# Inverse square roots by power on GpSimd, adjacency scaled once per graph, and the norms' last instruction on ScalarE

## The chip, the cores and the metric

The kernel runs on one core of one Trainium2 chip. The core has five engines that work at once, each through its own instructions in their order: TensorE (PE in the profile, its weight loads PEld), VectorE (DVE), ScalarE (ACT), GpSimd (POOL) and SyncE (SP), which here issues every DMA. What is measured is the device time of one launch in microseconds (us); less is better.

## The reference

64 graphs of N = 256 nodes with D = 128 features and a symmetric 0/1 adjacency with ones on its diagonal go through four layers. Every layer is followed by a residual and a layer norm without gain.

```
norm(v)  = (v - mean(v)) / sqrt(var(v) + 1e-5)            # over the 128 features
x1 = norm(x  + max_j adj[i,j] * relu(x_i (W1-W2) + x_j W2 + b))
x2 = norm(x1 + tanh([adj @ elu(x1 Win), elu(x1 Wnode), adj^T @ elu(x1 Wout)] @ Wupd + b))
A  = dinv_i * (adj + I) * dinv_j,   deg_i = sum_j adj[i,j] + 1,   dinv = deg^-1/2 where deg > 0, else 0
x3 = norm(x2 + A @ (elu(A @ (elu(elu(x2 W0 + b0)) W1) + b1) W2) + b2)
msg[i,j] = gelu(norm(x3_j Wa + x3_i Wb + b) * g1 + be1);  agg_i = sum_j adj[i,j] * msg[i,j]
z  = norm([x3, agg] @ W2 + b2) * g2 + be2
out = norm(x3 + z)
```

So there are five norms per graph: those that give x1, x2, x3 and out have no gain, the one that gives z has gain and offset. Layer 4 has in addition one inverse root for each message, a pair (i, j) of neighbours.

## The kernel before

Features or nodes lie on the 128 partitions; H = 2 halves of 128 nodes make a graph. The function `sparse` does the work; `general` is a second path that is entered only when a graph does not fit `sparse`'s tables, and in the measured runs it is not entered. A function such as `layernorm` is a Python generator: at each `yield` another may go on.

**Stages.** Four stages work on four successive graphs at once: `first` (layer 1), `second` (layer 2), `third` (layer 3, and the first four message tiles of layer 4) and `last` (the rest of layer 4 and the output). `together` takes steps of the four in turn, weighted by their number of steps: `STAGES = [(last, 34), (third, 34), (second, 14), (first, 44)]`. In the order in which the steps are taken, the instructions go into the engines' queues. All 64 graphs are unrolled.

**Layer 4.** Neighbours are packed into columns: WIDTH = 4800 columns for each half, cut into tiles of 1024, the last of 704, so that a graph has ten tiles (`TODO`). `sums_of` makes a tile: PE multiplies into `bigp` (L728), DVE adds `dT` into `pre` (L732), ACT squares (L736), PE sums over the features (L743), ACT writes the variances as `row` (L745), and SP sends `row` to a `line` in DRAM (L750). Each second tile (`GROUP = 2`) the group's variances come back spread over the partitions, as `vr` with 16 numbers on each of 128 (or 108) partitions (L762), and a mask `fu` (L764). `inverse_root` takes the square root on ACT and the reciprocal on DVE (L74, L75); L769 multiplies by the mask; L771 sends `vr` to `scale_line`. `last` fetches that, spread over all partitions, as `rs_s` (L828), two tiles ahead; DVE multiplies `pre` by it (L839), ACT takes the Gelu (L841), and DVE's `fold` adds it up (L492). There are 320 groups: five for each graph.

**Norms.** `layernorm` takes statistics on DVE (L171, L172), adds 1e-5 on DVE (L174), takes the root on ACT and the reciprocal on DVE (L74, L75) and then writes each half with one DVE instruction, subtract and multiply (L180), or two with a gain (L184, L185).

**Layer 3.** `layer_2` makes `deg` and `dinv` (root on ACT, reciprocal on DVE), adds the unit matrix to `aT` (L277), and in each of its two steps scales both halves of `hs` by `dinv` on DVE (L293) just ahead of the matrix products with `aT` (L296). The result is scaled by `dinv` of the other side in L308. `deg` comes from `dg`, a tile that `first` has left in `state`.

**ACT's tables.** ACT holds one set of functions at a time. Where the next activation needs another, an instruction ACT_TABLE_LOAD stands ahead of it, and the trace gives it the line of that activation: L74 (square root), L841 (Gelu), L194 and L198 (Exp of `elu`), L254 (Tanh).

Of the kernel before, what the change touches and what calls it, by code (L numbers as in the profile page):

```python
# [9 lines left out]
F32 = mybir.dt.float32  # L10
BF16 = mybir.dt.bfloat16
AF = mybir.ActivationFunctionType
# [31 lines left out]
def kernel(  # L44
# [26 lines left out]

    def inverse_root(t):

        nc.scalar.activation(t, t, AF.Sqrt)  # L74
        nc.vector.reciprocal(t, t)  # L75
# [81 lines left out]
    class Shared:  # L157
# [8 lines left out]
        def layernorm(self, dst, src, g=None, be=None):  # L166

            st = self.work.tile([P, H, 6], F32, name="st", bufs=4)
            mv = self.work.tile([P, H, 2], F32, name="mv", bufs=4)
            for h in range(H):  # L170
                nc.vector.bn_stats(st[:, h], src[:, h])  # L171
                nc.vector.bn_aggr(mv[:, h], st[:, h])  # L172
            rs = self.work.tile([P, H], F32, name="rs", bufs=4)
            nc.vector.tensor_scalar(rs, mv[:, :, 1], EPS, None, ALU.add)  # L174
            yield
            inverse_root(rs)
            yield
            for h in range(H):
                if g is None:
                    nc.vector.tensor_scalar(  # L180
                        dst[:, h], src[:, h], mv[:, h, 0:1], rs[:, h:h + 1], ALU.subtract, ALU.mult
                    )
                else:
                    nc.vector.scalar_tensor_tensor(dst[:, h], src[:, h], mv[:, h, 0:1], g, ALU.subtract, ALU.mult)  # L184
                    nc.vector.scalar_tensor_tensor(dst[:, h], dst[:, h], rs[:, h:h + 1], be, ALU.mult, ALU.add)  # L185
# [17 lines left out]
        def to_features(self, xn, name, bufs=None):  # L203

            pt = self.psum()
            for h in range(H):
                nc.tensor.transpose(pt[:, h * P:(h + 1) * P], xn[:, h], ident)
            t = self.state.tile([P, N], F32, name=name, **({"bufs": bufs} if bufs else {}))
            nc.scalar.copy(t, pt[:, :N])
            return t  # L210

# [49 lines left out]
        def layer_2(self, s, aT, deg_of):  # L261
# [3 lines left out]
            deg = work.tile([P, H], F32, name="deg")  # L265
            deg_of(deg)
            nc.vector.tensor_scalar(deg, deg, 1.0, None, ALU.add)
            pos = work.tile([P, H], F32, name="pos")
            nc.vector.tensor_scalar(pos, deg, 0.0, None, ALU.is_gt)
            dinv = work.tile([P, H], F32, name="dinv")  # L270
            nc.vector.tensor_scalar(dinv, deg, 1e-30, None, ALU.max)
            inverse_root(dinv)
            yield
            nc.vector.tensor_mul(dinv, dinv, pos)
            for h in range(H):
                blk = aT[:, h, h * P:(h + 1) * P]
                nc.vector.tensor_add(blk, blk, ident)  # L277
            yield
# [12 lines left out]
            for step in (1, 2):  # L291
                for h in range(H):
                    nc.vector.tensor_scalar(hs[:, h], hs[:, h], dinv[:, h:h + 1], None, ALU.mult)  # L293
# [60 lines left out]
    def sparse(ctx):  # L354
# [147 lines left out]
        def first(g, s):  # L502
# [40 lines left out]
            dg = state.tile([P, H], F32, name="dg", bufs=3)  # L543
            nc.vector.tensor_reduce(dg, pc, AX.X, ALU.add)
            s["dg"] = dg
# [172 lines left out]
        def sums_of(s, i):  # L718
# [50 lines left out]
            nc.vector.tensor_mul(vr[:rows], vr[:rows], fu[:rows])  # L769
# [12 lines left out]
        def third(g, s):  # L782

            dg = s["dg"]

            def deg_of(deg):
                nc.vector.tensor_scalar(deg, dg, 1.0 / N, None, ALU.mult)

            yield from sh.layer_2(s, s["aT"], deg_of)
# [105 lines left out]
    def general(ctx):  # L895
# [82 lines left out]
        def middle(g, s):  # L978
# [10 lines left out]
            def deg_of(deg):  # L989
                nc.vector.tensor_reduce(deg, an, AX.X, ALU.add)  # L990

            yield from sh.layer_1(s, an, aT, s["x1"])
            yield
            yield from sh.layer_2(s, aT, deg_of)
# [148 lines left out]
```

## Time and profile before

| | |
|---|---|
| median of 3 runs | 5732.73 us (5721.88 to 5733.99) |
| the profiled execution, its own time | 5731.62 us |
| its span, first to last instruction | 5729.7 us |
| mean granted TensorE clock | 0.862 |
| busy: PE, DVE, ACT | 4529.9, 4834.4, 4275.2 us |
| busy: POOL | 1.9 us, 10 instructions |

The page gives, for each engine, its busy time and share of the span; then the span in slices; the DMA queues; the chain of work that ended last, which is followed back from the last instruction; and the costliest groups of instructions. A group's line reads: line, engine, operation, output<-input, the shape, xcount, then busy us and mean ns of one, then the idle time of the engine just ahead of it, with what ended that. Busy shares are averages over stretches with different limits. So the table of stretches (the windows view), which gives each engine's busy time in any stretch of the span, is used as well, with the timeline and the list of waits (who waited for whom, us in total, times, longest).

### The profile page before, as it was taken

The numbers are of one execution on the slowest core, as the hardware profiler recorded it, in microseconds if no ns is written. First come the engines' busy times: TensorE is split into PE (matmuls) and PEld (weight loads), VectorE is DVE, ScalarE is ACT, GpSimd is POOL, SyncE is SP. The second block draws the span as 40 slices with busy tenths as digits, with TensorE's granted clock in tenths as the row PEclk, the third lists the DMA queues.
The fourth block names the chain that finished last, engine by engine and source line by source line (L and its number), as shares of the span: only waits on it lengthen the run. The fifth ranks groups of instructions, "written<-read, shape, count | busy, mean of one in ns | idle before, by whom it ended". The sixth has DMA issues, their size and how long they took to land.

```text
span 5729.7 us, 83531 instructions
## 1 busy us (share of the span) xinstructions
PE 4529.9 (79%) x27408; PEld 2508.7 (44%) x27408; DVE 4834.4 (84%) x14654; ACT 4275.2 (75%) x6485; POOL 1.9 (0%) x10
## 2 busy tenths in 40 slices
PE   5878878878778778788788788787887887877875
PEld 2444444444444444444444444444444444444443
DVE  6788888888888888888888888888888888888876
ACT  2577777777777777777777777777777777777785
POOL 0000000000000000000000000000000000000000
PEclk8888889889889889888898898898888887888986
DMA  0122222222212221221221222122212212221222
GB/s 22 44 70 63 62 63 72 62 63 66 69 57 70 65 63 63 72 63 62 63 72 62 63 65 70 59 68 65 63 62 72 64 62 63 69 66 60 68 65 74
DMA packets 292813, 365.15 MB, mean 64 GB/s; under 512 B 151952, under 2 KB 210448, under 8 KB 292368
## 3 DMA queue, kind: packets, MB, share of 16 engines
q1 hardware_dynamic: 292368, 359.73, 20.0%
q8 instruction: 217, 3.56, 0.3%
q14 instruction: 228, 1.87, 0.1%
HBM read 345.07 MB, written 14.53 MB: 63 GB/s over the span
## 4 chain that ended last, share of the span: by engine, by line
PE 52%; DVE 29%; ACT 11%; issue 4%; DMA 3%; SPq 0%; DVEq 0%; POOL 0%; ACTq 0%
PE bigp L665 11%; PE bigp L728 8%; DVE pre L839 6%; PE mm L860 5%; DVE lanes L492 4%; PE mm L743 4%; DVE hot L629 4%; DVE pre L732 4%; DVE sums L492 3%; PE bigp L681 3%; DMA rs_s<-scale_line 2%; PE mm L870 2%; PE mm L296 2%; PE mm L699 2%; PE mm L647 2%
## 5 line engine op out<-in xcount | busy, mean ns | idle before, releaser
L665 PE MATMUL bigp<-hot,q 128*128 128x512 fp8e4 (+1 forms) x3840 | 1052.3, 371 | 66.6 <-DVE lanes L492 52.6
L728 PE MATMUL bigp<-hot,c 128*128 128x512 fp8e4 (+1 forms) x3840 | 928.8, 372 | 140.2 <-DVE pre L732 140.2
L732 DVE TENSOR_TENSOR pre<-bigp,dT 128x512 f32<-128x512 f32 (+6 forms) x1664 | 846.3, 530 | 37.8 <-PE bigp L728 33.5
L492 DVE TENSOR_TENSOR lanes<-bigp,lanes 128x512 f32<-128x512 f32 (+6 forms) x1536 | 772.7, 503 | 94.6 <-PE bigp L681 86.9
L839 DVE TENSOR_TENSOR pre<-pre,rs_s 128x1024 f32<-128x1024 f32 (+1 forms) x640 | 732.9, 1150 | 48.6 <-DMA rs_s<-scale_line 48.0
L736 ACT ACTIVATE sq<-pre 128x1024 f32<-128x1024 f32 (+1 forms) x640 | 638.5, 998 | 169.9 <-DVE pre L732 163.9
L841 ACT ACT_TABLE_LOAD x535 | 686.4, 1283 | 9.5
L492 DVE TENSOR_TENSOR sums<-pre,sums 128x1024 f32<-128x1024 f32 (+6 forms) x1024 | 628.8, 614 | 41.2 <-ACT pre L841 40.7
L745 ACT ACTIVATE row<-mm,eps_t 128x256 f32<-128x256 f32 (+1 forms) x640 | 289.6, 453 | 476.9 <-PE mm L743 476.7
L841 ACT ACTIVATE pre<-pre,be,g 128x1024 f32<-128x1024 f32 (+1 forms) x512 | 594.2, 1172 | 57.8 <-DVE pre L839 53.0
L743 PE MATMUL mm<-sq,ones 128*32 128x256 f32 (+1 forms) x5120 | 482.9, 440 | 135.2 <-ACT sq L736 135.2
L74 ACT ACT_TABLE_LOAD x445 | 570.9, 1283 | 7.5
L728 PEld LDWEIGHTS <-c 128*128 128x128 bf16 x3840 | 331.2, 98 | 550.5 <-issue 136.1
L665 PEld LDWEIGHTS <-q 128*128 128x128 bf16 x3840 | 310.8, 97 | 392.6 <-issue 112.0
L296 PE MATMUL mm<-aT,hs 128*128 128x256 f32 x512 | 232.3, 600 | 316.1 <-DVE hs L293 214.8
L629 DVE TENSOR_SCALAR hot<-rank 128x512 fp8e4<-128x512 bf16 (+5 forms) x1536 | 440.5, 348 | 0.0
L681 PEld LDWEIGHTS <-pick 42*128 42x128 bf16 x2944 | 155.8, 95 | 481.5 <-issue 474.2
L296 PEld LDWEIGHTS mm<-aT,hs 128*128 128x128 f32 x512 | 135.6, 293 | 425.8 <-issue 316.1
L860 PE MATMUL mm<-w3u,sums 128*128 128x128 f32 x2048 | 296.7, 289 | 18.4 <-DVE sums L492 16.1
L194 ACT ACT_TABLE_LOAD x221 | 283.5, 1283 | 3.9
L681 PE MATMUL bigp<-lack,pick 42*128 42x36 bf16 (+16 forms) x2944 | 285.7, 187 | 0.0
L860 PEld LDWEIGHTS mm<-w3u,sums 128*128 128x128 f32 x2048 | 254.5, 195 | 37.3 <-issue 17.6
(226 smaller groups left out, 7132.6 us busy)
## 6 DMA issues: line engine op xcount, KB each, us to landing
rs_s<-scale_line SPq DMA_DIRECT2D x512, 512.0 KB
rs_s<-scale_line SPq DMA_DIRECT2D x128, 352.0 KB
an<-in_adj SPq DMA_DIRECT2D x64, 256.0 KB
x<-in_x SPq DMA_DIRECT2D x64, 128.0 KB
line<-row SPq DMA_DIRECT2D x512, 4.0 KB
out<-o SPq DMA_DIRECT2D x64, 128.0 KB
fu<-fulls SPq DMA_DIRECT2D x192, 4.0 KB
vr<-line SPq DMA_DIRECT2D x192, 8.0 KB
```

Source lines behind the costliest of these rows:

```text
L74: nc.scalar.activation(t, t, AF.Sqrt)
L492: nc.vector.tensor_tensor(lanes[:, :k, :w], src[:, i:i + k], lanes[:, :k, :w], op)
L629: nc.vector.tensor_scalar(hot[:, :, at:at + w], rank[:, :, :w], s0 + i + 1.0 - FAR, None, ALU.is_equal, saturate=False)
L665: nc.tensor.matmul(pt[:, :tl], q3[:, i, h], hot[:, h, t0:t0 + tl], start=i == 0, stop=False)
L681: nc.tensor.matmul(o_, l_, r_, start=False, stop=i == len(todo) - 1)
L728: nc.tensor.matmul(pt[:, :bl], c3[:, k, h], hot[:, h, t0 + b:t0 + b + bl], start=k == 0, stop=k == 2)
L732: nc.vector.tensor_add(block(pre[:, b:], n, w, at), block(pt, n, w, at), widen(dT[:, h, :w], n))
L736: nc.scalar.activation(sq[:, :tl], pre[:, :tl], AF.Square)
L743: nc.tensor.matmul(pr[q * Q:(q + 1) * Q, :tl // 4], ones[:, :Q], v4[:, :, q], start=True, stop=True)
L839: nc.vector.tensor_mul(pre[:, :tl], pre[:, :tl], rs[:, :tl])
L841: nc.scalar.activation(msg[:, :tl], pre[:, :tl], AF.Gelu, bias=be3, scale=g3)
L860: nc.tensor.matmul(pt[:, cols], lanes[:, k, cols], w3u[:, 1], start=k == 0, stop=False)
```

## The change

`inverse_root` becomes one GpSimd instruction: `t` to the power of a tile `mhalf`, which holds -0.5. It serves the scales (`vr`, [128, 16] or [108, 16]) and `dinv` ([128, 2]). The products with the masks, `fu` and `pos`, go to GpSimd too. `dinv` is now made in `first`, by `inverse_root_of`, and kept in `state` with four buffers. `layer_2` scales the two halves of `aT` once by `dinv`, after the unit matrix is added, and no longer scales `hs` in each step. `layernorm` no longer uses `inverse_root`: the root on ACT takes 1e-5 as its bias, DVE takes the reciprocal, and, without a gain, an offset -mean * rs; then ACT writes each half as Identity with that scale and offset. Its `yield`s move; without a gain there is one more.

```diff
+    mhalf = consts.tile([P, 16], F32, name="mhalf")
+    nc.vector.memset(mhalf, -0.5)
+
     def inverse_root(t):
 
-        nc.scalar.activation(t, t, AF.Sqrt)
-        nc.vector.reciprocal(t, t)
+        nc.gpsimd.tensor_tensor(t, t, mhalf[:t.shape[0], :t.free_size()], ALU.pow)
...
             for h in range(H):
                 nc.vector.bn_stats(st[:, h], src[:, h])
                 nc.vector.bn_aggr(mv[:, h], st[:, h])
+            yield
             rs = self.work.tile([P, H], F32, name="rs", bufs=4)
-            nc.vector.tensor_scalar(rs, mv[:, :, 1], EPS, None, ALU.add)
-            yield
-            inverse_root(rs)
-            yield
+            nc.scalar.activation(rs, mv[:, :, 1], AF.Sqrt, bias=eps_t)
+            yield
+            nc.vector.reciprocal(rs, rs)
+            if g is None:
+                off = self.work.tile([P, H], F32, name="off", bufs=4)
+                nc.vector.scalar_tensor_tensor(off, mv[:, :, 0], -1.0, rs, ALU.mult, ALU.mult)
+                yield
             for h in range(H):
                 if g is None:
-                    nc.vector.tensor_scalar(
-                        dst[:, h], src[:, h], mv[:, h, 0:1], rs[:, h:h + 1], ALU.subtract, ALU.mult
+                    nc.scalar.activation(
+                        dst[:, h], src[:, h], AF.Identity, bias=off[:, h:h + 1], scale=rs[:, h:h + 1]
                     )
...
+        def inverse_root_of(self, deg, bufs):
+
+            nc.vector.tensor_scalar(deg, deg, 1.0, None, ALU.add)
+            pos = self.work.tile([P, H], F32, name="pos")
+            nc.vector.tensor_scalar(pos, deg, 0.0, None, ALU.is_gt)
+            dinv = self.state.tile([P, H], F32, name="dinv", bufs=bufs)
+            nc.vector.tensor_scalar(dinv, deg, 1e-30, None, ALU.max)
+            inverse_root(dinv)
+            nc.gpsimd.tensor_mul(dinv, dinv, pos)
+            return dinv
...
-        def layer_2(self, s, aT, deg_of):
+        def layer_2(self, s, aT, dinv_of):
...
-            deg = work.tile([P, H], F32, name="deg")
-            deg_of(deg)
-            nc.vector.tensor_scalar(deg, deg, 1.0, None, ALU.add)
-            pos = work.tile([P, H], F32, name="pos")
-            nc.vector.tensor_scalar(pos, deg, 0.0, None, ALU.is_gt)
-            dinv = work.tile([P, H], F32, name="dinv")
-            nc.vector.tensor_scalar(dinv, deg, 1e-30, None, ALU.max)
-            inverse_root(dinv)
-            yield
-            nc.vector.tensor_mul(dinv, dinv, pos)
+            dinv = dinv_of()
+            yield
             for h in range(H):
                 blk = aT[:, h, h * P:(h + 1) * P]
                 nc.vector.tensor_add(blk, blk, ident)
+            for h in range(H):
+                nc.vector.tensor_scalar(aT[:, h], aT[:, h], dinv[:, h:h + 1], None, ALU.mult)
...
             for step in (1, 2):
-                for h in range(H):
-                    nc.vector.tensor_scalar(hs[:, h], hs[:, h], dinv[:, h:h + 1], None, ALU.mult)
                 pa = psum()
...
-            dg = state.tile([P, H], F32, name="dg", bufs=3)
+            dg = work.tile([P, H], F32, name="dg")
             nc.vector.tensor_reduce(dg, pc, AX.X, ALU.add)
-            s["dg"] = dg
+            nc.vector.tensor_scalar(dg, dg, 1.0 / N, None, ALU.mult)
+            s["dinv"] = sh.inverse_root_of(dg, 4)
...
             inverse_root(vr[:rows])
-            nc.vector.tensor_mul(vr[:rows], vr[:rows], fu[:rows])
+            nc.gpsimd.tensor_mul(vr[:rows], vr[:rows], fu[:rows])
...
-            yield from sh.layer_2(s, s["aT"], deg_of)
+            yield from sh.layer_2(s, s["aT"], lambda: s["dinv"])
```

`general` gets a `dinv_of` of its own in the same manner.

More of the change, by code (lines that the diff above doesn't have):

```diff
@@ L782, in third @@
         def third(g, s):
-            dg = s["dg"]
-            def deg_of(deg):
-                nc.vector.tensor_scalar(deg, dg, 1.0 / N, None, ALU.mult)
-            yield from sh.layer_2(s, s["aT"], deg_of)
+            yield from sh.layer_2(s, s["aT"], lambda: s["dinv"])
             yield
@@ L987, in middle, with dinv_of @@
             yield
-            def deg_of(deg):
+            def dinv_of():
+                deg = work.tile([P, H], F32, name="deg")
                 nc.vector.tensor_reduce(deg, an, AX.X, ALU.add)
+                return sh.inverse_root_of(deg, 1)
             yield from sh.layer_1(s, an, aT, s["x1"])
             yield
-            yield from sh.layer_2(s, aT, deg_of)
+            yield from sh.layer_2(s, aT, dinv_of)
             yield
```

## Prediction

> **What bounds the kernel now.** I read the page's busy shares first, then the table of stretches over one graph, then the lists of groups and of waits.
>
> ```profile
> PE 4529.9 (79%) x27408; PEld 2508.7 (44%) x27408; DVE 4834.4 (84%) x14654; ACT 4275.2 (75%) x6485; POOL 1.9 (0%) x10
> ```
> No engine is full over the span, and POOL is free. The stretches show why (us; busy us of PE, PEld, DVE, ACT, POOL; then clock and DMA):
>
> ```profile
> 1982.00:2034.00 52.00, 50.66 (x320) 29.10 (x320) 45.25 (x135) 35.20 (x51) 0.00 (x0) 0.97 0.26 82
> 2034.00:2067.00 33.00, 18.39 (x110) 8.60 (x109) 29.29 (x93) 30.98 (x50) 0.00 (x0) 0.83 0.13 43
> 2067.00:2122.00 55.00, 52.61 (x331) 30.34 (x332) 46.68 (x144) 36.28 (x55) 0.00 (x0) 0.95 0.25 78
> 2122.00:2156.00 34.00, 17.49 (x98) 8.66 (x96) 28.32 (x86) 31.53 (x50) 0.00 (x0) 0.75 0.15 43
> ```
> Two graphs, 87 us each. Each has a **PE stretch** of some 53.5 us (PE 97% busy, DVE 86%, ACT 67%) and an **elementwise stretch** of some 33.5 us (ACT 93%, DVE 86%, PE half idle). What ACT and DVE save counts almost only in the second; in the first DVE has some 7 us to spare.
>
> ```profile
> L841 ACT ACT_TABLE_LOAD x535 | 686.4, 1283 | 9.5
> L839 DVE TENSOR_TENSOR pre<-pre,rs_s 128x1024 f32<-128x1024 f32 x512 | 622.3, 1216 | 22.8 <-DMA rs_s<-scale_line 22.2
> L74 ACT ACT_TABLE_LOAD x445 | 570.9, 1283 | 7.5
> L492 DVE TENSOR_TENSOR sums<-pre,sums 128x1024 f32<-128x1024 f32 x256 | 312.0, 1219 | 37.0 <-ACT pre L841 36.9
> L194 ACT ACT_TABLE_LOAD x221 | 283.5, 1283 | 3.9
> ```
> Table loads, 1236 in all, take 1586 us of ACT, more than a third. The long DVE instructions L839 and L492 read two tiles from SBUF.
>
> ```profile
> PE mm L296 <- DVE hs L293: 214.8, 67, 8.7
> PE mm L207 <- DVE x L180: 107.8, 63, 5.2
> DVE pre L839 <- DMA rs_s<-scale_line: 48.0, 57, 4.2
> SPq L771 <- DVE vr L769: 565.2, 101, 7.6
> ```
> PE waits for the scaling that goes (L293) and for the norm's last instruction (L180); DVE seldom waits for scales; SP, in order, stands long behind the scales' last product.
>
> **What the Trainium skill says.** "ScalarE: Activation LUTs", section "What ACT_TABLE_LOAD costs", gives 1283 ns for a load whatever the set; the trace has 1283 on each. "SBUF — State Buffer", section "Who interferes with whom": GpSimd and DVE share one pair of SBUF ports as an exclusive lock; a DVE instruction with two SBUF inputs, or in a two-port mode, and a GpSimd instruction that reads SBUF block each other, the later one for the whole of the earlier. With ten POOL instructions the trace can't show that. It decides my forecast.
>
> **The change, part by part.** Counts are over 64 graphs; 5 groups and 5 norms a graph.
>
> *ACT, roots gone.* 320 roots of vr at 0.21 us and 64 of dinv at 0.20: -81 us. With them go loads. I took ACT's activations in the trace's order, each with its set (Tanh is at home with Exp and Gelu), and counted the switches: 1236, as recorded. Without the vr and dinv roots 767 remain. So -469 x 1.283 = -602 us.
>
> *ACT, norms added.* 512 Identity on 128x128 with two operands per partition. Nearest row L841: 1241 ns for 1024 columns, 966 for 704, 0.86 ns a column; at 128 that is 0.47 us, so +241. It can hardly cost under 0.36 (a 128x256 copy, L209) or over 0.6. The norms' roots get a bias operand, at most 0.09 x 320 = +29, as L841 against L736 (two operands, +0.19). ACT in sum: 4275 - 413 = 3862 us.
>
> *DVE.* Gone: reciprocal and mask of vr 78.5 + 52.9 = 131 us; L174 51; L180 512 x 0.339 = 173; dinv's reciprocal and product 20; L293 256 x 0.281 = 72. Added: scaling aT, 128 instructions at L560's 0.347 (bounds 0.27 to 0.45) = 44; `off`, 256 at L174's 0.16 = 41. Sum 4834 - 362 = 4472, before any stall. dinv's three small instructions and the 1/N move from `third` to `first`, the count unchanged.
>
> *POOL.* 320 powers of 16 numbers on each partition, 64 of two, 384 products. No row shows a power. Low end: DVE's product of that shape, 0.17. For the middle: "GPSIMD Engine Reference", section "Performance pitfalls for Q7 kernels", gives 4 cycles for each step of a dependent fp32 chain, and its specifications 1.2 GHz. A power as logarithm, product and exponential is by my estimate 40 to 60 such steps: 160 to 240 cycles a number, 2.1 to 3.2 us for 16. I take 2.7, and 0.3 for the product. High end, with nothing overlapped in longer code: 6. POOL is then busy 320 x 3.0 + 64 x 0.9 = 1018 us, 18%: not a bound. It would be one at 16 us.
>
> *The scales' path and SP.* No DMA is added. L771 now waits for POOL, and behind it SP's queue holds the next `row`, `fu`, `rs_s` and output DMAs as before. In the timeline a vr, issued at 2002.5, met its table load at 2004.7, its root at 2006.0, reciprocal 2006.4, product 2006.9, L771 at 2007.0. On POOL nothing is queued ahead: landing, 2.7, 0.3, about level with that. Cost nothing, as long as `rs_s` is fetched two tiles ahead; with a power of 6 us that cover is gone.
>
> *The lock.* A hold of 3.0 us (power and product) laid over DVE's recorded order at each of the 320 landings (2.3 us after issue; the longest such wait of SP is 2.8) lasts past the start of DVE's next instruction with two SBUF inputs by 2.3 us on average: 740 us in all. At 1.5 us it is 0.85 each, at 6 us 5.3, at 0.3 almost nothing.
>
> *The sum for one graph.* **Elementwise stretch**: two groups, norms of x1 and out. ACT: a vr root with its load and the load after it, another root alone, -3.0; four Identity +1.9: -1.1. DVE: L180 -1.3, vr -0.8, L174 -0.3, L293 -1.0, off +0.3: -3.1, and stalls 2 x 2.3 = +4.6: +1.5. Which of the two ends last there I weigh 60 DVE to 40 ACT: 0.9 - 0.4 = +0.5. **PE stretch**: three groups: DVE -1.2 (vr), -1.4 (L180), -0.5 (L174), -0.3 (dinv), +0.3 (off), +0.7 (aT), stalls +6.9: +4.5, so DVE goes from 46 to 50.5 of 53.5 us. PE waits there for DVE to empty its PSUM tiles; a quarter comes through, +1.1. **Waits of PE**: L296 no longer waits for L293 behind other DVE work, -0.5 (214.8 us / 64 = 3.4, nearly all in stretches where PE is not last). Behind L180's place, L207 waits for `off` and then for ACT's turn, where Gelus of 1.2 us and loads stand ahead: some +0.2 net, bounds 0 to 1.5. Total +1.3 us, x 64 = +83: 5731.6 + 83 = **5815 us**. The profiled execution is 1.1 us under the median of the runs shown, so the same is meant for the median.
>
> By the same terms, with a stall s for each group the sum is 2.0 s - 3.2 us: nothing changes at s = 1.6, a hold of some 2.3 us.
>
> **The rivals.** (1) *A short hold: faster.* POOL keeps the ports only while it reads its 16 numbers, and computes without them. Then s is about 0, and the sum is -3.2 us a graph, -200; but half of what one engine gives up, the next in the stretch takes (DVE and ACT are within 3 us of each other), so some -100: 5630, at most 5530. For it: ACT is the fullest in the elementwise stretch, and loads and roots leave it. It decides below a hold of 2.3 us. Against it: the skill's sentence on the whole instruction. (2) *A long power*, 6 us or more: s = 5.3, +7 us a graph, `rs_s` late too: 6180 or above. Nothing in the profile excludes it. (3) *The hop through ACT*: L207's wait grows by 1.5 us for three norms a graph; with the short hold it eats the gain, about 5735; with the long one 5900. (4) *The loads stay.* The order is remade, and the norms' roots fall between Gelu and Exp so that over 1000 loads remain: ACT gains under 200 us, worth 0.4 x 3 x 64 = 70 us at most; with the hold 5880.
>
> **How the numbers follow.** About 0.2% is what a measurement of this kernel can tell from no change. The hold of 2.3 us or longer with a power near 2.7, hops and loads in the ways above: 0.50, nearly all slower, 5750 to 5900. Short hold 0.36, of which 0.32 faster and 0.04 level. Long power 0.07. Hop eating a short hold's gain 0.07, level to faster. So faster 0.37, same 0.07, slower 0.56. The likeliest is 5815, its own range 5750 to 5900. The range for 8 in 10 takes in most of the short hold and leaves out the long power: 5590 to 5930.
>
> **What would show it.** Right: ACT table loads near 770 and ACT's busy time near 3860; POOL at some 1000 us; L839 and the `sums` folds of L492 longer than 1216 ns on average, or idle time before them, together by some hundred us; the elementwise stretches not shorter, in spite of ACT's lower share. Wrong: a power over 4 us, waits for `rs_s` in hundreds of us, or DVE's two-input instructions at their old lengths without new gaps; then the lock was not the term that I make it, and the kernel is faster.

## The result, and the profile after

| | before | after |
|---|---|---|
| median | 5729.03 us (4 runs) | 6005.45 us (6002.55 to 6009.44, 4 runs) |
| ratio after / before | | 1.0484 [1.0466, 1.0502] |
| span of the profiled execution | 5729.7 us | 6006.0 us |
| mean granted TensorE clock | 0.862 | 0.835 |
| ACT's table loads | 1236 | 639 |

The changed kernel is 276 us slower, 4.3 us for each graph. Its line numbers are some three to ten higher: L844 is the product with `rs_s` (L839 before), L846 the Gelu, L501 the `fold`, L186 the norm's last instruction, L77 the power, L779 and L781 the mask's product and the scales' output, L738 and L742 the sums' matrix products and their emptying. The busy shares of the page:

```profile
PE 4649.4 (77%) x27408; PEld 2543.1 (42%) x27408; DVE 4609.6 (77%) x13183; ACT 3689.5 (61%) x6016; POOL 1213.0 (20%) x778
```
ACT lost 586 us and DVE 225, and no engine is near full. PE's busy time grew by 120 us for the same number of products, at a lower granted clock; its share still fell, as that of every engine but POOL. So much of the time that came is waiting, and the next view is the groups, with shapes kept apart (busy us, mean ns of one, then the idle time ahead of them and what ended it):

```profile
L844 DVE TENSOR_TENSOR pre<-pre,rs_s 128x1024 f32<-128x1024 f32 x512 | 624.2, 1219 | 531.9 <-DMA rs_s<-scale_line 531.7
L77 POOL TENSOR_TENSOR vr<-vr,mhalf 128x16 f32<-128x16 f32 x192 | 577.6, 3009 | 2213.0 <-DMA vr<-line 2213.0
L846 ACT ACT_TABLE_LOAD x315 | 404.1, 1283 | 5.6
L501 DVE TENSOR_TENSOR sums<-pre,sums 128x1024 f32<-128x1024 f32 x256 | 311.7, 1218 | 38.6 <-ACT pre L846 38.2
L186 ACT ACTIVATE x<-y,off,rs 128x128 f32<-128x128 f32 x256 | 110.8, 480 | 5.7 <-DVE off L182 5.7
```
The two long DVE instructions with two SBUF inputs have kept their lengths (1219 and 1218 ns; 1216 and 1219 before). What is new is the idle time ahead of the first: 531.7 us of waiting for scales, where it was 22.2. The list of waits (who, for whom; us in total, times, longest) puts all shapes together:

```profile
DVE pre L844 <- DMA rs_s<-scale_line: 546.9, 202, 6.9
PEld mm L213 <- ACT x L186: 280.1, 132, 7.8
PE mm L213 <- ACT x L186: 224.8, 66, 7.2
PE mm L305 <- DVE hs L207: 149.7, 68, 8.3
```
In the kernel before, the prediction's lines have PE's own wait for x (107.8); that of its loads was

```profile
PEld mm L207 <- DVE x L180: 145.4, 66, 5.7
```
Three things to see. DVE's wait for scales grew from 48.0 to 546.9 us. PE's wait ahead of the transposes of x grew as well: PE and its loads together, which overlap, from 253 us (for DVE) to 505 (for ACT). The wait ahead of the products with the adjacency fell from 214.8 to 149.7. Which of them costs time can't be read from such a list. The chain that ended last gives a first hint; first of the kernel before, then of the changed one:

```profile
PE 52%; DVE 29%; ACT 11%; issue 4%; DMA 3%; SPq 0%; DVEq 0%; POOL 0%; ACTq 0%
```
```profile
issue 43%; PE 17%; POOL 14%; DMA 10%; DVE 8%; ACT 7%; SPq 0%; POOLq 0%; ACTq 0%; DVEq 0%
```
An engine that is busy for 20% of the span carries 14% of the chain, where it had nothing before. It is no more than a hint: "issue" is time for which the profile shows no wait, and it is 43% of this chain.

### The profile page after: what moved, and what is told of

The parts are those of the page before. It is cut to its first block, busy times and chain, and to the rows that moved or that the text cites. A ratio compares the mean times of both kernels' runs of the same rounds, so it can differ in the third digit from the quotient of the medians.

```text
span 6006.0 us, 82321 instructions
## 1 busy us (share of the span) xinstructions
PE 4649.4 (77%) x27408; PEld 2543.1 (42%) x27408; DVE 4609.6 (77%) x13183; ACT 3689.5 (61%) x6016; POOL 1213.0 (20%) x778
## 4 chain that ended last, share of the span: by engine, by line
issue 43%; PE 17%; POOL 14%; DMA 10%; DVE 8%; ACT 7%; SPq 0%; POOLq 0%; ACTq 0%; DVEq 0%
POOL vr L77 12%; DMA rs_s<-scale_line 5%; PE bigp L675 4%; DVE pre L844 3%; PE bigp L738 3%; PE mm L753 2%; POOL vr L779 2%; DMA scale_line<-vr 2%; DMA vr<-line 2%; DVE hot L639 2%; DMA line<-row 1%; ACT sq L746 1%; ACT pre L846 1%; ACT L200 1%; PE bigp L691 1%
## 5 line engine op out<-in xcount | busy, mean ns | idle before, releaser
L77 POOL TENSOR_TENSOR vr<-vr,mhalf 128x16 f32<-128x16 f32 (+1 forms) x320 | 1019.5, 3186 | 4015.6 <-DMA vr<-line 4015.6
L738 PE MATMUL bigp<-hot,c 128*128 128x512 fp8e4 (+1 forms) x3840 | 951.5, 374 | 275.5 <-DVE pre L742 228.6
L844 DVE TENSOR_TENSOR pre<-pre,rs_s 128x1024 f32<-128x1024 f32 (+1 forms) x640 | 732.1, 1152 | 547.2 <-DMA rs_s<-scale_line 546.9
L675 PE MATMUL bigp<-hot,q 128*128 128x512 fp8e4 (+1 forms) x3840 | 1038.9, 370 | 9.6 <-DVE q L508 8.2
L501 DVE TENSOR_TENSOR lanes<-bigp,lanes 128x512 f32<-128x512 f32 (+6 forms) x1536 | 775.2, 505 | 94.4 <-PE bigp L691 76.9
L742 DVE TENSOR_TENSOR pre<-bigp,dT 128x512 f32<-128x512 f32 (+6 forms) x1664 | 836.1, 525 | 14.6 <-PE bigp L738 12.4
L846 ACT ACTIVATE pre<-pre,be,g 128x1024 f32<-128x1024 f32 (+1 forms) x512 | 594.9, 1173 | 372.6 <-DVE pre L844 369.7
L501 DVE TENSOR_TENSOR sums<-pre,sums 128x1024 f32<-128x1024 f32 (+6 forms) x1024 | 630.7, 616 | 102.8 <-ACT pre L846 98.1
L738 PEld LDWEIGHTS <-c 128*128 128x128 bf16 x3840 | 352.9, 99 | 693.0 <-issue 297.7
L305 PE MATMUL mm<-aT,hs 128*128 128x256 f32 x512 | 242.3, 624 | 149.7 <-DVE hs L207 149.7
L213 PE MATMUL mm<-ident,x 128*128 128x128 f32 x512 | 165.5, 378 | 227.0 <-ACT x L186 224.8
```

The lines of the kernel that those rows point to most:

```text
L77: nc.gpsimd.tensor_tensor(t, t, mhalf[:t.shape[0], :t.free_size()], ALU.pow)
L501: nc.vector.tensor_tensor(lanes[:, :k, :w], src[:, i:i + k], lanes[:, :k, :w], op)
L675: nc.tensor.matmul(pt[:, :tl], q3[:, i, h], hot[:, h, t0:t0 + tl], start=i == 0, stop=False)
L738: nc.tensor.matmul(pt[:, :bl], c3[:, k, h], hot[:, h, t0 + b:t0 + b + bl], start=k == 0, stop=k == 2)
L742: nc.vector.tensor_add(block(pre[:, b:], n, w, at), block(pt, n, w, at), widen(dT[:, h, :w], n))
L844: nc.vector.tensor_mul(pre[:, :tl], pre[:, :tl], rs[:, :tl])
```

## The experiments

Short diffs are against the kernel named. Each ratio is to runs of the kernel before on the same chip; the medians of the kernel before differ by up to 8 us from chip to chip, and differences in us between two experiments on different chips are good to about that. The waits that the text gives come from each kernel's own list of waits; line numbers shift by a few from kernel to kernel.

A remark on **order** first, since it serves as a control. The front part says that instructions go into the queues in the order of the stages' steps. That isn't the whole of it: the order is made anew when the program is built, and a local edit can change it in places that it doesn't touch. e4 moves nothing but the scales' root and mask, and changes no `yield` and no matrix product. Compared place by place, PE's queue leaves that of before at its 714th product, and of the first 6000 places 5025 hold the same product (line, tiles and shape). So most comparisons here change an operation and the order with it. Three pairs don't: e5 and before (the queues of PE, ACT and SP alike throughout, DVE's but for two constants set at the start), e4 and e9, the kernel after and e13 (PE, DVE, ACT and SP the same throughout, POOL's but for the one instruction). These three carry the conclusions.

### The parts alone: e4, e6, e7, and the whole without one part: e3

e4, from before, the scales' root and mask:

```diff
-            inverse_root(vr[:rows])
-            nc.vector.tensor_mul(vr[:rows], vr[:rows], fu[:rows])
+            nc.gpsimd.tensor_tensor(vr[:rows], vr[:rows], mhalf[:rows], ALU.pow)
+            nc.gpsimd.tensor_mul(vr[:rows], vr[:rows], fu[:rows])
```


> The kernel before, with the root and the mask of vr alone on GpSimd, nothing else changed. Power theory: most of the loss comes with it, 5900-6000, DVE's wait for rs_s from 48 to over 350 us. Schedule theory: the path is level and ACT loses some 350 loads, so 5640-5760. Port theory: 320 holds of 3 us lengthen DVE's instructions with two SBUF inputs or the idle time ahead of them, 5850 or more without waits for rs_s.

Measured: 5954.29 us, 1.0385 [1.0368, 1.0402]; DVE's waits for `rs_s` are 648.9 us.

e6, from before, `layernorm` as in the kernel after, nothing else:

> The kernel before with the norms alone changed: root with bias on ACT, offset on DVE, two Identity on ACT, the yields moved. Hop theory: PE's wait for x behind the transposes grows from 108 to near 290 us, as in the run without GpSimd's root, and most of that run's 185 us is here: 5850-5920. Adjacency theory (the loss is in dinv and aT): 5710-5770, since DVE loses 170 us of work and ACT gains 270.

Measured: 5937.33 us, 1.0376 [1.0358, 1.0393]. ACT has 4432.9 us (74.7% of 5937). PE waits longest for `hs`, 543.6 us at the place that took 214.8 before. The waits for x, which the hop theory has growing, did not grow: 245 us of PE and its loads together, against 253.

e7, from before, the adjacency scaled once, `dinv` made as before:

```diff
                 nc.vector.tensor_add(blk, blk, ident)
+            for h in range(H):
+                nc.vector.tensor_scalar(aT[:, h], aT[:, h], dinv[:, h:h + 1], None, ALU.mult)
...
-                for h in range(H):
-                    nc.vector.tensor_scalar(hs[:, h], hs[:, h], dinv[:, h:h + 1], None, ALU.mult)
```


> The kernel before with aT scaled once by dinv and the scaling of hs in each step gone; dinv is made where it was, root on ACT. Hop theory: no loss, 5690-5750, since the products no longer wait for L293 (215 us of PE's waits). Adjacency theory: 5800-5900. Order theory: somewhere between 5720 and 5850, because the queues' order is made anew.

Measured: 5690.88 us, 0.9946 [0.9930, 0.9963]. **Faster than both kernels, by half a per cent against the one before.** Its wait for `hs` ahead of the adjacency's products is 188.5 us.

e3, the kernel after, but the scales' root back on ACT, reciprocal and mask on DVE:

```diff
-            inverse_root(vr[:rows])
-            nc.gpsimd.tensor_mul(vr[:rows], vr[:rows], fu[:rows])
+            nc.scalar.activation(vr[:rows], vr[:rows], AF.Sqrt)
+            nc.vector.reciprocal(vr[:rows], vr[:rows])
+            nc.vector.tensor_mul(vr[:rows], vr[:rows], fu[:rows])
```


> The changed kernel with the root of vr back on ACT and reciprocal and mask back on DVE; dinv, aT and norms stay changed. Power theory: the path loses the 3.0 us, DVE's wait for rs_s falls under 150 us, 5680-5780. Schedule theory: vr to scale_line took 5.3 us before and 5.2 us after, so the path is level and the scales stay late: 5950-6050, wait over 350 us; ACT gets its loads back (over 1000).

Measured: 5917.64 us, 1.0313 [1.0293, 1.0333]; its waits for `rs_s` are 90.6 us, those for x from ACT 646 (PE 288.7, its loads 356.9), and PE's for `hs` 327.1, against 149.7 in the kernel after. The waits for scales are the power theory's, the time is neither theory's.

What follows: two parts lose and one gains. 3.85 + 3.76 - 0.54 is 7.1%, and all together lose 4.84, so the parts don't add. With the root on ACT the late scales are gone and most of the loss stays, in yet another order: late scales aren't the only thing that can cost time here.

### Does GpSimd slow VectorE? e5

From before; nobody reads `idle`, and the scales go on through ACT and DVE as they did:

```diff
+            idle = big.tile([P, PIECE], F32, name="idle")
+            nc.gpsimd.tensor_add(idle[:rows], one16[:rows], fu[:rows])
+            nc.gpsimd.tensor_tensor(idle[:rows], idle[:rows], mhalf[:rows], ALU.pow)
             inverse_root(vr[:rows])
```


> The kernel before, and in addition on GpSimd, for each of the 320 groups, a sum and a power of 16 numbers on a scratch tile that nobody reads; they start when the mask fu has landed. The scales stay on ACT and DVE. Port theory: the 320 powers of 3 us hold DVE up, 2 to 4 us a graph, 5850-6000, with DVE's two-input instructions longer or gaps ahead of them. Power theory (late scales) and order theory (what costs is the other order in the queues, which were tuned for the kernel before): 5710-5760.

Measured: 5726.37 us, 1.0001 [0.9993, 1.0009]. From its groups by shape:

```profile
L774 POOL TENSOR_TENSOR idle<-idle,mhalf 128x16 f32<-128x16 f32 x192 | 560.1, 2917 | 15.1
L846 DVE TENSOR_TENSOR pre<-pre,rs_s 128x1024 f32<-128x1024 f32 x512 | 621.9, 1215 | 22.0 <-DMA rs_s<-scale_line 21.1
```
320 powers of 2.9 us run beside a program in the same order, and DVE's instruction with two SBUF inputs takes 1215 ns (1216 before), with the same 22 us of idle time ahead. The powers of e5 start at another moment than those of the change, so the trace of the kernel after has to say the same: of DVE's 768 instructions of 1024 columns with two SBUF inputs (L844 and the `sums` of L501), 136 began while a power was running. They took 1214 ns on average, the 505 with no GpSimd instruction beside them 1221. No cost to VectorE of a power that runs beside it can be measured.

### Steps and weights: e1, e2, e8

e1, after, the weights raised by the step that each stage has gained: `STAGES = [(last, 35), (third, 35), (second, 15), (first, 45)]`.

> The changed kernel, with the stages' weights raised by one each (35, 35, 15, 45), the number of steps that they have now. Schedule theory: the norm's added yield gives each stage one step more than its weight, so what third does after x3's norm slips by one step of 34 (some 2.7 us of 92) against last of the next graph, and the scales of the first tiles come late. Then DVE's wait for rs_s falls from 547 us to under 200, and the time from 6006 to 5700-5820. Power theory: the scales are late because a power takes 3.0 us in their path; the weights change nothing, 5960-6040, wait near 547. Port theory (GpSimd and VectorE hold each other up): nothing either.

Measured: 6016.39 us, 1.0501 [1.0483, 1.0518]; `rs_s` waits 652.4 us.

e2, after, without the `yield` behind `off`.

> The changed kernel without the one yield that it adds to each norm without a gain: off and the two Identity instructions go out in one step, weights as they were. Schedule theory: as with the new weights, 5700-5820, DVE's wait for rs_s under 200 us. Power theory and port theory: 5960-6040.

Measured: 5977.72 us, 1.0432 [1.0414, 1.0449]; `rs_s` waits 367.1 us.

e8, before, with one more `yield` in each norm without gain and no instruction changed.

> The kernel before with one more yield ahead of the last instruction of each norm without a gain; no instruction is changed, only the order in which the steps of the four stages are taken. Order theory: 5780-5900, the kernel loses 1 to 3% by this alone. The other theories: 5715-5760.

Measured: 5746.72 us, 1.0040 [1.0026, 1.0054].

Steps account for some half per cent either way; the weights are not the cause. e8 shows something more: without one instruction changed, the other order has 1030 table loads in place of 1236, ACT is busy for 4007.2 us in place of 4275.2, and the kernel is not faster. There the relief of ACT bought no time.

### The length of the power: e4 against e9, the kernel after against e13

e9 is e4, and e13 the kernel after, with `ALU.mult` where `ALU.pow` stood. They leave the root out of the scales, so the scales hold other numbers. In each pair only the length of one GpSimd instruction differs. That other numbers do not change times by themselves is assumed; in e13 the Gelus of 1024 columns take 1241 ns (1242 in the kernel after) and DVE's product 1220 (1219).

> The kernel of e4 (the scales' root and mask on GpSimd, all else as before) with the power replaced by a product of the same two tiles: the root is left out of the scales. GpSimd then takes about 0.2 us where it took 3.0, and ScalarE is relieved of the same 320 roots. Theory L (e4 loses because the power keeps the scales on GpSimd for 3 us, and VectorE has them late): near the kernel before, 5700 to 5770 us, and VectorE's waits for rs_s fall from 649 to under 150 us. Theory Q (e4 loses because the program's queues are put in another order once ScalarE no longer has these roots, and the multiplications stand too near the rows that they wait for): still above 5850 us, rs_s waits above 350 us although the path is 3 us shorter.

Measured: 5667.74 us, 0.9894 [0.9878, 0.9911], lower than either theory had it. The waits for scales of e4, then of e9:

```profile
DVE pre L842 <- DMA rs_s<-scale_line: 648.9, 151, 6.6
```
```profile
DVE pre L842 <- DMA rs_s<-scale_line: 287.6, 129, 4.8
```
361 us of waiting go, and 287 us of time. POOL's instruction went from 3201 to 505 ns on average. The waits that I expected to stay under 150 us are 288, so this order had scales late by itself.

> The kernel after, with the scales' power replaced by a product of the same two tiles (the root is left out of the scales): GpSimd takes 0.2 us where it took 3.0, and the instructions of all other queues stand in the same order as in the kernel after. Theory L (late scales cost the whole change about what they cost e4, 5.0% between e4 and e9): 5700 to 5800 us, rs_s waits down from 547 to under 200 us. Theory H (with the norms on ScalarE, the hop is what holds the period, and the late scales lie under it): over 5880 us, waits for x from ScalarE stay at 505 us or grow.

Measured: 5608.99 us, 0.9787 [0.9772, 0.9802]: **396 us less than the kernel after**, and 2.1% faster than before. Both theories had the time too high. Its groups by shape:

```profile
L844 DVE TENSOR_TENSOR pre<-pre,rs_s 128x1024 f32<-128x1024 f32 x512 | 624.6, 1220 | 84.1 <-DMA rs_s<-scale_line 81.7
L778 POOL TENSOR_TENSOR vr<-vr,mhalf 128x16 f32<-128x16 f32 x192 | 59.5, 310 | 2438.2 <-DMA vr<-line 2438.2
```
The idle time ahead of L844 fell from 531.9 to 84.1 us for an instruction that stands at the same place. One tile shows how. These are lines of the timeline, with others left out (start us, duration us, engine, instruction; in brackets its engine's idle time ahead, and what ended it), first of the kernel after, then of e13, for the same tile in the same order:

```profile
2125.83 0.53 SPq L760 DMA_DIRECT2D line<-row  x1
2129.95 0.33 SPq L772 DMA_DIRECT2D vr<-line  x1
...
2131.66 3.54 POOL L77 TENSOR_TENSOR vr<-vr,mhalf 128x16 f32<-128x16 f32 x1 [10.35 <-DMA vr<-line]
2135.29 0.22 POOL L779 TENSOR_TENSOR vr<-vr,fu 128x16 f32<-128x16 f32 x1
2135.53 0.33 SPq L781 DMA_DIRECT2D scale_line<-vr  x1
2136.96 0.79 SPq L833 DMA_DIRECT2D rs_s<-scale_line  x2
2141.18 1.22 DVE L844 TENSOR_TENSOR pre<-pre,rs_s 128x1024 f32<-128x1024 f32 x1 [4.44 <-DMA rs_s<-scale_line]
```
```profile
1993.03 0.33 SPq L772 DMA_DIRECT2D vr<-line  x1
...
1994.70 0.83 POOL L778 TENSOR_TENSOR vr<-vr,mhalf 128x16 f32<-128x16 f32 x1 [10.38 <-DMA vr<-line]
1995.61 0.22 POOL L779 TENSOR_TENSOR vr<-vr,fu 128x16 f32<-128x16 f32 x1
1995.85 0.33 SPq L781 DMA_DIRECT2D scale_line<-vr  x1
1997.28 0.79 SPq L833 DMA_DIRECT2D rs_s<-scale_line  x2
2001.11 1.22 DVE L844 TENSOR_TENSOR pre<-pre,rs_s 128x1024 f32<-128x1024 f32 x1 [0.52 <-DMA rs_s<-scale_line]
```
From the start of the power to the start of the multiplication it is 9.52 us with the power and 6.41 with the product. The power is 2.71 us longer, and DVE stands still for 4.44 us instead of 0.52. The variances are on their way for all of that time: SP issues the write at 2125.83, so the scales take 15.35 us from there, and 11.81 of these are not the power.

Where this graph pays, the table of stretches shows, cut at the same multiplications (tile 0, 2, 4, 8, and tile 0 of the next graph; from, to, length, busy us of PE, PEld, DVE, ACT, POOL, then clock). The kernel after:

```profile
2128.80:2141.20 12.40, 6.66 (x32) 2.75 (x31) 7.38 (x13) 7.33 (x11) 3.76 (x2) 0.60 0.37 104
2141.20:2171.00 29.80, 20.76 (x95) 10.66 (x95) 24.37 (x77) 20.31 (x36) 5.92 (x5) 0.65 0.11 34
2171.00:2194.00 23.00, 21.21 (x138) 12.49 (x138) 18.44 (x47) 15.31 (x24) 6.60 (x4) 1.00 0.31 99
2194.00:2219.80 25.80, 23.07 (x166) 12.69 (x164) 21.23 (x69) 13.86 (x23) 3.12 (x2) 1.00 0.16 44
```
e13:

```profile
1991.80:2001.10 9.30, 3.02 (x16) 1.55 (x14) 7.37 (x12) 8.64 (x12) 1.04 (x2) 0.83 0.43 141
2001.10:2031.00 29.90, 23.08 (x115) 11.95 (x113) 24.52 (x77) 21.20 (x39) 2.63 (x6) 0.65 0.13 38
2031.00:2051.30 20.30, 18.49 (x126) 10.80 (x126) 18.44 (x47) 14.09 (x22) 1.95 (x2) 1.00 0.37 109
2051.30:2076.90 25.60, 25.48 (x178) 14.30 (x177) 21.37 (x70) 13.64 (x25) 0.44 (x2) 1.00 0.14 39
```
Between tiles 0 and 2 the kernel after loses 3.1 us, between 4 and 8 it loses 2.7, elsewhere nothing: 5.9 of the 6.2 us a graph (396 / 64). These two stretches each end at a multiplication whose scales come last, and each is longer by about one power. The other three powers of this graph cost nothing. Over all 64 graphs, from the starts of these multiplications in the two traces, the losses are 2.8 us, 0.8 (tiles 2 to 4), 2.3 and 0.3 on average: most of it, but not all, lies in the same two stretches. What the lower granted clock of the kernel after (0.835 against 0.855, and 124 us more busy time of PE) has in this is not separated.

### The norms' last instruction on ScalarE: e10, e11, e18

e10, from before: root and its steps as they were, DVE makes `off`, ACT writes the result.

```diff
             inverse_root(rs)
+            if g is None:
+                off = self.work.tile([P, H], F32, name="off", bufs=4)
+                nc.vector.scalar_tensor_tensor(off, mv[:, :, 0], -1.0, rs, ALU.mult, ALU.mult)
             yield
...
-                    nc.vector.tensor_scalar(
-                        dst[:, h], src[:, h], mv[:, h, 0:1], rs[:, h:h + 1], ALU.subtract, ALU.mult
+                    nc.scalar.activation(
+                        dst[:, h], src[:, h], AF.Identity, bias=off[:, h:h + 1], scale=rs[:, h:h + 1]
                     )
```


> Before, with one thing of the norms changed: the last instruction of the norms without gain runs on ScalarE as scale and offset (VectorE makes the offset); the root, its two steps and everything else stay as they were. Theory H (the hop through ScalarE's queue is what e6's 3.8% are made of): most of it stays, 5850 to 5950 us, TensorE and its weight loads wait over 250 us for x from ScalarE, or VectorE's hs comes later as in e6 (over 450 us). Theory S (the bias in the root and the step that moved ahead of it cost it, through the order of the queues): 5730 to 5800 us.

Measured: 6033.96 us, 1.0533 [1.0515, 1.0552]. This one edit costs more than the whole change. Its waits:

```profile
PEld mm L210 <- ACT x L183: 327.7, 132, 8.0
PE mm L210 <- ACT x L183: 276.7, 66, 7.5
```
604 us for x where before had 253: +351, against +305 us of time. But PE's wait for `hs` grew too, from 214.8 to 394.4 us, so the waits don't say which of the two it is.

e11, from before: the root takes EPS as its bias and the sum on DVE goes; the two `yield`s stand ahead of the root and ahead of the reciprocal; the last instruction stays on DVE.

> Before, with the other half of the norms' change: the root takes EPS as its bias on ScalarE, the sum on VectorE is gone and the step stands ahead of the root, and the last instruction stays on VectorE. VectorE loses 384 sums of two elements a partition. Theory H: no loss, 5690 to 5750 us. Theory S: 5800 to 5950 us, with hs or rs_s waits of over 400 us.

Measured: 5811.79 us, 1.0154 [1.0136, 1.0172], within theory S's times; PE's wait for `hs` is 391.6 us. So both theories hold a part: the hop's half costs more than H asked, and the other half costs 1.5% without any hop. Each half alone and both together (e6) give 1.5, 5.3 and 3.8%: these don't add either.

e18 is e13 with the norms of before, so it has neither the scales' nor the degrees' roots on ACT, and the scales' root is left out here too.

> The kernel of e13 (5609 us; the scales' root left out of both) with the norms as in the kernel before: sum, root and reciprocal with the last instruction on VectorE. Theory I (the hop's price depends on ScalarE's load: with the scales' and the degrees' roots gone it is cheap, and VectorE's 320 us less are worth more): slower than e13, 5640 to 5720 us. Theory H (the hop costs 3.8 to 5.3% anywhere): faster than e13, 5350 to 5450 us.

Measured: 5629.35 us, 0.9826 [0.9808, 0.9845], so the norms' part *gains* 20 us there (5629.35 to 5608.99), 0.4% by the two ratios. e13 waits 640 us for x from ACT (PE 296.9, its loads 342.8), more than e10, and is the fastest kernel of all. A wait in the list is not a bill: PE can wait at L213 and still not be what ends the stretch.

So the hop has no price that holds from one program to the next; in e6 even its waits are missing. Where ACT still has the roots (75% busy in e6 and e10), the norms' part loses 3.8 to 5.3%; where they are gone (65% in e18), it gains. That is theory I's sign, if less than it asked. In all of these the order of the queues differs too, so how much is ACT's load and how much the order stays **open**.

### Starting the scales earlier, or in smaller pieces: e16, e17, e14, e15

e16 is e4, and e17 the kernel after, with `AHEAD = 5` instead of 4.

> The kernel of e4 (5954 us) with the sums started five tiles ahead of their use in place of four, everything else as in e4 (power of 16 elements, pairs of tiles; seven buffers of pre as before, so two are left for what is in use). Theory L: the scales are a tile (about 9 us) earlier where they were up to 6.6 us late; rs_s waits fall under 150 us, and the time to 5700 to 5800 us, if the buffers of pre suffice. If they don't, TensorE's sums wait for a free pre and the time stays above 5850 us with small rs_s waits.

Measured: 5777.65 us, 1.0086 [1.0070, 1.0102]; `rs_s` waits 402.9 us. It gives back 177 us, against 287 for the shorter instruction in e9; the time is theory L's, the waits are well above it.

> The kernel after (6005 us) with the sums started five tiles ahead of their use in place of four, nothing else. Theory L (the power's length on the scales' path is the whole loss, 396 us between after and e13, and a tile's earlier start hides it): 5650 to 5800 us, rs_s waits from 547 to under 300 us, about 44 to 60% of the 396 us given back if it goes as in e16 (177 of 287). Theory H (the norms' hop holds the period): above 5900 us.

Measured: 6061.56 us, 1.0573 [1.0547, 1.0599]. Its wait:

```profile
DVE pre L844 <- DMA rs_s<-scale_line: 619.8, 233, 6.6
```
The time is theory H's, but not its reason: the hop was to hold the period while the scales come early, and the waits for scales grew instead, from 546.9 to 619.8 us. The sums start a tile earlier, but in the order made for this program the scales are late again.

e14 is e4, and e15 is e7 with e4's edit, with scales made for each tile by itself (`GROUP = 1`, `PIECE = 8`, the weights raised by the new steps).

> The kernel of e4 (5954 us) with scales made for each tile by itself instead of for two: powers of 8 elements a partition, 640 of them, at about 1.6 us, and the first tile of a pair no longer waits for the second one's row; 960 more transfers are issued on SP, and ScalarE has nothing more to do. Theory L (lateness): the power is 1.4 us shorter and half of the scales start a tile earlier, so 5680 to 5780 us, rs_s waits under 250 us. Theory P (what counts is GpSimd's share or the number of small transfers): 5950 us or more, since GpSimd is as busy and the transfers double.

Measured: 5883.97 us, 1.0265 [1.0241, 1.0289]; `rs_s` waits 491.8 us. The power takes 1965 ns on average (median 1636, as expected), and PE's waits for `hs` grew from e4's 190.3 to 604.4 us. Neither theory's number.

> The candidate: e14 with the adjacency scaled once, as in e7. If both parts add: e14's ratio times 0.995. Theory L: 5650 to 5750 us. Theory P: 5920 us or more.

Measured: 5976.36 us, 1.0429 [1.0414, 1.0443]. The adjacency's gain in e7 turned into a loss of 1.6% beside e14. The time is theory P's; e15 doesn't show that its reason is.

### The degrees' root alone on GpSimd: e12

e12 is e7 with `nc.gpsimd.tensor_tensor(dinv, dinv, mhalf[:, :H], ALU.pow)` where `inverse_root(dinv)` stood.

> The kernel of e7 (adjacency scaled once, 5690.9 us) with the root of dinv alone as a power on GpSimd, at the place where it stood. 64 roots and up to some 120 table loads leave ScalarE (up to 160 us of its time), a power of 0.7 us takes their place on the path of layer 2. Theory of the ends of stages (TensorE waits for the adjacency 64 times; a load and a root of 1.5 us and a reciprocal go, 0.7 us and a hop come): 5660 to 5700 us. Theory Q (any relief of ScalarE remakes the queues at random): anything from 5660 to 5900 us, with waits at places that this edit doesn't touch.

Measured: 5743.90 us, 1.0031 [1.0018, 1.0044]: 53 us slower than e7, though ACT gives up 162 us and no wait at `dinv`'s own place grew (that for `hs` is 192.2 us against 188.5). It lies in theory Q's range, and nothing here shows why.

## Why the prediction was right or wrong

The direction was right, by the wrong mechanism, and the time, 6005 us, lies outside of the range (5590 to 5930).

- **The lock** is the step that decided the forecast, and it failed. It put 740 us of stalls on DVE; e5 measured none (1.0001). The step rested on the Trainium skill, "SBUF — State Buffer". By its sections "Who interferes with whom" and "SBUF: two separate sides", a GpSimd instruction that reads SBUF and a DVE instruction with two SBUF inputs contend, and the one that starts first has the shared ports for its whole length. For a power of 16 numbers on each partition the measurement decides against that on DVE's side: the 136 instructions that began during a power were not longer (1214 against 1221 ns). The rival of a short hold was right about DVE and wrong about the end: without the stall the kernel was not faster.
- **The scales' path**: "Cost nothing, as long as `rs_s` is fetched two tiles ahead". This is the step that hid the real loss, 396 us with the queues unmoved (after against e13). I compared one old path (root on ACT, with its load, reciprocal and product) with the new one and found them level. Averages that I worked out from the trace's records agree: 5.28 us from the issue of `vr` to the end of the product before, 5.22 after. What the average hides is both ends of the path, at the tiles that pay. At tile 2, DVE multiplied 14.0 us after ACT had finished the group's second row before, without waiting; after, it was ready after 10.0 and waited 4.5 us more. I had taken that place as given. And for the same tile the way from the row to the issue of `rs_s` grew from 8.0 to 10.3 us, 1.7 of it ahead of the fetch of `vr`, so that it was not level there. At tiles 0 and 8 the way was 0.6 us shorter and 0.1 longer, DVE was ready 3.5 and 2.8 us earlier, and it waits 1.5 and 2.2 us; elsewhere hardly at all. Whether DVE is ready earlier because work has left ACT and DVE or because of the order is not separated. The sign was on my list ("waits for `rs_s` in hundreds of us"), but reserved for a power over 4 us, and with the wrong consequence ("the kernel is faster").
- **The power** was sized well: 2.7 us taken, 2.99 the median after (3.19 on average), 2.91 the median in e5. The product is 0.22 us at the median and 0.42 on average, against 0.3. POOL: 1018 us forecast, 1213 measured.
- **ACT** lost more than I counted: 3862 forecast, 3689.5 measured. The term is the loads: 767 counted in the old order, 639 in the new one; 128 x 1.283 is 164 of the 172 us. The rival of loads that stay did not come. The Identity was right (0.47 against 0.48 us).
- **DVE**: 362 us less forecast; summed over its instructions in the trace it is 370. The page's busy time fell by only 225, since it counts overlapping instructions once.
- **L207's hop**, +0.2 us a graph with bounds of 0 to 1.5: the waits grew by 252 us, 3.9 a graph (PE and its loads together, which overlap). As a cost of time it can't be given one number: +305 us in e10, -20 between e18 and e13. The rival that made it 1.5 us for three norms (3 x 1.5 x 64 = 288 us) has the size of e10's loss, but e10 has no GpSimd powers, and in e6 the waits for x did not grow.
- **L296**: -0.5 us a graph. e7, which holds this and DVE's saving on it, gives 0.0054 x 5729 / 64 = -0.5. About right, with some luck, since e7's queues stand in another order too.
- **The order of the queues** was in my text only as a rival on table loads. It is the larger omission: a local edit moves much else with it. A step without instructions costs 0.4% (e8), and e11, which shifts two steps and drops a sum of two elements, 1.5%.

What the experiments show in the place of my sum: with no stall it says -3.2 us a graph, and the change without the power's length has -1.9 (e13, 2.1% faster). The term of the scales' path, which I put at nothing, is +6.2 us a graph, and turns that into 4.8% slower. So the direction of my forecast was luck. Why ScalarE's 586 us less bring no more than those 2.1% is open in part: the order that came with it was never tried with the old operations, and e8, where the order alone takes 268 us from ScalarE, is 0.4% slower.

## What to carry to other kernels

When work moves from a busy engine to an idle one, compare not its busy time but its latency with the slack of whoever waits at the end of its path: here some 2.7 us more at two places a graph outweighed 586 us less on ScalarE. Take that slack tile by tile, since an average over tiles was level and hid it. To separate the length of an operation from the order that is made around it, swap it for a shorter one of the same form and see that all queues stay alike; only such a pair prices it. Take from this change the part that adds no hop between engines, the adjacency scaled once (e7, 0.9946), and measure it again in your own kernel: beside e14 it lost 1.6%.

## What the runs showed of the hardware

- 320 GpSimd powers of 2.9 us, each reading and writing 128x16 or 108x16 in SBUF, don't change DVE's two-input instructions (1215 against 1216 ns) or the time (1.0001 [0.9993, 1.0009], e5). It is POOL's own instructions that stretch, from a median of 2.99 up to 5.67 us for the power and from 0.22 up to 1.29 for the product. In the kernel after, the 76 products of `vr` and `fu` that began while a DVE instruction with two SBUF inputs was running took 0.90 us on average, the other 244 took 0.27. So a running DVE instruction goes with a longer GpSimd instruction, and a running power doesn't go with a longer DVE instruction.
- The power has a fixed part and one for each number on a partition. The shortest took 0.70 us for 2 numbers and 2.90 for 16 (kernel after), and 1.63 for 8 (e14): by my estimate from these, 0.38 us and 0.16 for each number. A product of the same 16 numbers took 0.22.
- The granted clock is lower over the span with the late scales, 0.835 against 0.855 in e13, and the same 27408 matrix products take 4649 us of PE in the kernel after and 4525 in e13. No rule comes out of these runs: in the first stretch of the windows above the clock is 0.60 with PE busy for 54% of the stretch (kernel after) and 0.83 with 32% (e13), and e2, with PE busy for no larger a share than in the kernel after (76 and 77%), has 0.857.
